# Projecting the context values of the second pair of units one slot earlier, into the other accumulator pool

## The chip, the cores and the metric

The kernel runs on one core of a Trainium2 chip. The time is that of one execution on the device, in microseconds; the time before is the median of three runs. All data are 32-bit floats.

The core has engines that each work through their own queue of instructions in order: TensorE (PE in the profile, with its weight loads under PEld), VectorE (DVE), ScalarE (ACT), GpSimd (POOL), and SyncE (SP), which here only hands out DMA transfers. PE writes its products into banks of accumulator memory (PSUM); a bank can be given to a new product only when DVE or ACT has copied the old one out.

## The reference

One transformer block on `x` of shape (2, 1024, 256) and a context `cond` of shape (2, 154, 192), with 16 heads of 64:

```python
h = _layernorm(x, ln1_g, ln1_b)
x = _attention(h, h, sa_wq, sa_wk, sa_wv, sa_wo, sa_bo) + x
h = _layernorm(x, ln2_g, ln2_b)
x = _attention(h, cond_emb, ca_wq, ca_wk, ca_wv, ca_wo, ca_bo) + x
h = _layernorm(x, ln3_g, ln3_b)
p = h @ ff_w1 + ff_b1
a, gate = (p[..., :D_FF], p[..., D_FF:])
h = a * jax.nn.gelu(gate, approximate=False) @ ff_w2 + ff_b2
return h + x
```

`_attention(xq, xkv, ...)` projects queries from `xq` and keys and values from `xkv`, takes the softmax of the scaled products per head, weighs the values and multiplies by `wo`. The change lies in the second call, context attention: the keys and values come from the 154 rows of the context, and the value projection is `v = cond_emb @ ca_wv`.

## The kernel before, in words

The whole order of work is written out by hand: the instructions go to each engine's queue in the order in which the Python code calls them, and a framework adds the semaphore waits. Three stages follow each other: self attention, context attention (from about 697 us of the span), and the gated feed-forward layer (from about 895 us).

**Units and slots.** A unit is a batch and a pair of heads; there are 16 (`units`, eight per batch). Context attention works on a unit in three slots, since its eight tiles of 128 tokens are taken as 3 + 3 + 2 (`CG`), so there are 48 slots, numbered `c` from 0; `ui, n = divmod(c, 3)` are unit and part. The slots around the change are 5 to 11: slot 5 is the last of unit 1, slots 6, 7 and 8 are unit 2, slots 9, 10 and 11 are unit 3.

**What a slot issues.** `cross_first(c)` puts the scores on PE (L873, tile `sc`) and the row maxima on DVE (L879, `neg`); then what waited in the list `stores` is flushed, that is, copies out of accumulators; then `then()` puts the exponents on ACT (L890, six or four of them, which need the maxima). The call before's `late` puts a reciprocal on DVE (L898, `rden`) and the division on POOL (L901). `cross_drain(c)` transposes the result of slot `c - 2` on DVE (L917). Then comes what is special to the slot. With `n == 0` from unit 3 on, the queries of the next unit are projected (L369, `pq_ca`) and copied out by ACT in the next slot (L384, `q_ca`); in slot 6 two pieces of self attention's output projection stand there instead (L500, `py_sa`, added to `x` by DVE, L507). With `n == 1`, `cross_weigh(c)` weighs the values of the unit two before (L953, `poc`), and DVE copies the sums out (L967, `o_ca`). `cross_regroup` moves the transposed weights to where that product wants them, with eight DMAs on SP (L934).

**Context values.** `context_values(b, pr)` (L820) serves two units at a time, with 256 columns. For the first two pairs it clears a part of the buffer on DVE (L829, `held_v`), multiplies the context by the weights on PE (two matmuls, four passes in the trace, L833, `pv_ca`), and leaves a store that copies the product with two instructions on ACT (L843) and asks for six DMAs (two at L845, which need the copies, and four at L850). The weights (`ca_wv`) are loaded by one DMA on SP (L123). Before, this is called for units 2, 4, 6 and so on in the slot with `n == 1`, ahead of `cross_weigh`.

**Two pools of banks.** `mm_tile` and `sum_tile` each hand out two banks in turn; `ps_s` holds two double banks for scores. `cross_values` (L937) takes the first two quarters of a unit (part 0) in banks of `sum_tile` and the last two (part 1) in banks of `mm_tile`:

```python
po = {a4: (mm_tile if a2 else sum_tile)(f"poc_{ui}_{a4}") for a4 in quarters}
```

So in slot 7 the product `pv_ca` and the two quarters of part 1 all come from `mm_tile`, which has two banks.

Of the kernel before, what the change touches and what calls it, by code (L numbers as in the profile page):

```python
# [18 lines left out]
def tile_transformer_block(ctx: ExitStack, tc: tile.TileContext, a: dict, out: bass.AP):  # L19
# [11 lines left out]
    HP = NPAIR // NQ  # L31
# [38 lines left out]
    def mm_tile(name):  # L70
        return ps_m.tile([P, HB], F32, tag="mm", name=name)
# [54 lines left out]
    def load_slice(name, c0, n, p):  # L126

        own = w[name][:, c0:c0 + n]
        if p != HR:
            return load_rows(wpool, name[3:], f"{name}_{c0}", own, p)  # L130
        tag = "wk" if name == "ca_wq" and c0 // P % 2 else name[3:]
        t = wpool.tile([P, NH, n], F32, tag=tag, name=f"{name}_{c0}")
        for r0 in range(0, P, HR):
            nc.sync.dma_start(out=t[r0:r0 + HR], in_=own.rearrange("(c p) f -> p c f", p=HR))
        return t
# [3 lines left out]
    def load_weights(kind, pr, what):  # L139
        if what != "v":  # L140
            wsl[kind, pr, what] = load_slice(f"{kind}_w{what}", pr * P, P, HR)
        elif pr % 2 == 0:
            wsl[kind, pr, what] = load_slice(
                f"{kind}_w{what}", pr * P, VC, HR if kind == "sa" else CC)
# [446 lines left out]
    def run(piece):  # L591
        done = piece()
        if done is not None:
            (adds if getattr(done, "adds", False) else stores).append(done)
# [6 lines left out]
    def run_work(n, n_side, bank=None, n_sum=0):  # L601

        while n > 0 and work:
            n -= work[0].banks
            run(work.pop(0))
        for _ in range(min(n_side, len(side))):
            needs_bank, needs, fn = side[0]  # L610
            if needs_bank and not bank and n <= 0 or not added.issuperset(needs):
                break
            if needs_bank and not bank:
                n -= 1
            spare["bank"] = bank or mm_tile
            run(fn)
            side.pop(0)
        if not spare["turned"]:
            flush(slow)
        for i in range(min(max(n, 0) + n_sum, len(outs))):  # L620
            spare["out"] = mm_tile if i < n else sum_tile
            run(outs.pop(0))
# [4 lines left out]
    units = [(b, pr) for b in range(B) for pr in range(NPAIR)]  # L627
# [144 lines left out]
    CG = [(t, min(TG, NT - t)) for t in range(0, NT, TG)]  # L772
# [44 lines left out]
                    )  # L817
        return lambda: nc.scalar.copy(ends[:, f:f + n], pe[:, :n])

    def context_values(b, pr):  # L820

        i = (b * NPAIR + pr) // 2
        if i < 2:
            v = vs["own", i] = held_v[:, i].rearrange("p t d -> p (t d)").rearrange(
                "p (n d) -> p n d", d=VC)
            nc.vector.memset(v[:, NM:, :], 0.0)  # L829
        v = vs["ca", b, pr // 2] = vs["own", i % 2]  # L830
        pv = mm_tile(f"pv_ca{b}_{pr}")
        for c in range(2):
            nc.tensor.matmul(  # L833
                pv[:, :VC], lhsT=ctxT[:, c, b * TP:b * TP + P],
                rhs=wsl["ca", pr, "v"][:, c, :], start=(c == 0), stop=(c == 1),
            )
        half, c0 = divmod(pr * P, DA // 2)
        last = (2 * b + half) * KB

        def store():  # L840
            for n in range(NM):
                own = slice(n * QG, (n + 1) * QG)
                nc.scalar.copy(v[own, n, :], pv[own, :VC])  # L843
            later.insert(0, lambda: [
                nc.sync.dma_start(  # L845
                    out=v[(1 - n) * QG:(2 - n) * QG, n, :], in_=v[n * QG:(n + 1) * QG, n, :])
                for n in range(NM)
            ])
            later.insert(1, lambda: [
                nc.sync.dma_start(  # L850
                    out=v[a4 * KB:(a4 + 1) * KB, NM + a4 % 2, :],
                    in_=ends[last:last + KB, c0:c0 + VC])
                for a4 in range(P // KB)
            ])

        return store
# [409 lines left out]
    with tc.manual_schedule():  # L1266
# [59 lines left out]
        for p in range(SA):  # L1326
# [21 lines left out]
            ui, n = divmod(p, 2 * SH)  # L1348
# [6 lines left out]
            if hg == LAG:  # L1355
                f = (ui - NPAIR // 2 - 1) * EC
# [4 lines left out]
                if n == SH + LAG and ui in (0, 1, NU - 1):  # L1361

                    pr = {0: 2, 1: 4, NU - 1: 6}[ui]
# [3 lines left out]
        for c in range(CA):  # L1367
            if c == 1:
                pTc["ring"] = pt_.tile(
                    [P, 2 * NK, QH // 2], F32, tag="pT", name="pT_ca"  # L1370
                ).rearrange("p a b -> p (a b)")[:, :3 * 2 * NB * NT * KB].rearrange(
                    "p (u n j q) -> p u n j q", u=3, n=NB, j=2)
            if c == SH + 1:
                out_pieces("sa", B - 1, NQ - 1, out_order("sa"))
            if c == SH + 1:

                w1, w2, parts = hold_gated()
                add_biases("ca", 0)
                others = later[:] + [lambda: None] * (len(parts) - len(later))
                later[:] = [fn for pair in zip(parts, others) for fn in pair] + others[len(parts):]  # L1380
            ui, n = divmod(c, len(CG))
            nxt = units[ui + 1] if ui + 1 < NU else None
            if n == 0:
                cross_beside(ui)
            elif n == 1 and 1 <= ui < NU - 3:
                load_weights("ca", units[ui + 3][1], "q")
            elif n == 2 and nxt and ui:
                load_weights("ca", nxt[1], "v")
            flush(adds)
            then = cross_first(c)  # L1390
            if c < 2:
                reciprocals(SA - 2 + c)
            flush(stores)
            if c == 1:
                turn_group(SA - 2, 0)
                turn_group(SA - 2, 1)
                scale_rows(SA - 1, 0, 4)
            flush(lates)
            lates.append(then())
            if c == 0:  # L1400
                join(SA - 1)
                turn_group(SA - 3, 1)
            if c == 2:
                turn_group(SA - 1, 0)
                turn_group(SA - 1, 1)
            cross_drain(c)
            if c == 0:
                run(lambda: self_values(2 * NU - 2, 1))
            elif c == 1:
                run(lambda: cross_queries(*units[2]))  # L1410
            elif c == 2:
                run(lambda: cross_queries(*units[3], bank=sum_tile, tag="KT"))
            elif c == 3:
                run(lambda: self_values(2 * NU - 1, 0))
            elif c == 4:
                run(lambda: self_values(2 * NU - 1, 1))
            elif n == 0 and ui:
                if nxt and ui > 2:
                    run(lambda: cross_queries(*nxt))
                else:  # L1420
                    run_work(2, 0)
                run_work(0, 1)
            elif n == 1:

                spare["turned"] = True
                run_work(0, 1, sum_tile if outs else None)
                flush(stores)
                run_work(0, 0, n_sum=1)
                if ui % 2 == 0:
                    run(lambda: context_values(*units[ui]))  # L1430
                run_work(1, 0)
                flush(adds)
                flush(slow)
                flush(stores)
                cross_weigh(c)
            elif n == 2:
                run_work(0, ui != HP, sum_tile if ui == HP + 1 else None)
                if c == SH + 1:
                    run_work(2, 0)
                elif ui == HP:  # L1440
                    wo["ca"] = const.tile([P, NPAIR, D], F32, tag="wo", name="ca_wo")
                    later[1:1] = [lambda i=i: nc.sync.dma_start(
                        out=wo["ca"][:, i, :], in_=w["ca_wo"][i * P:(i + 1) * P, :])
                        for i in range(NPAIR)]
            flush(slow)
            cross_regroup(c)
            for _ in range(min(1 if ui in (HP, HP + 1) else 2, len(later))):
                later.pop(0)()
            if c == CA - 22:
                weighted = [fn for n in range(4) for fn in weight_sums(n)]  # L1450
            if CA - 22 <= c < CA - 10:
                weighted.pop(0)()
            elif c >= CA - 3:
                for n in {CA - 3: (4,), CA - 2: (5, 6), CA - 1: (7,)}[c]:
                    weight_sums(n)[0]()
            if c == CA - 5:
                token_sums(0)
# [7 lines left out]
        for k in range(2 * FU):  # L1465
            c = CA + k
# [17 lines left out]
            while n_left > 0 and sums:  # L1484
                fn, n = sums.pop(0)
# [51 lines left out]
```

## Time and profile before

| | |
|---|---|
| median of 3 runs | 1069.95 us (1069.39 to 1070.63) |
| the profiled execution | 1071.75 us |
| its span (first to last instruction) | 1069.1 us |
| PE busy | 1057.3 us (99%) |
| DVE, ACT, POOL busy | 882.9, 645.3, 774.8 us |
| granted PE clock | 1.0 over the span |

The profile of one execution lists for each engine its instructions in order of time, with the idle time before a group of them and what ended it; the chain of waits follows the work that ended last backwards; and the view of waits adds up who waited for whom. The span leaves out 2.65 us of the profiled execution's own time, and that execution was 1.80 us above the median. Only differences within the span are used below.

### The profile page before, as it was taken

The numbers are of one execution on the slowest core, as the hardware profiler recorded it, in microseconds if no ns is written. First come the engines' busy times: TensorE is split into PE (matmuls) and PEld (weight loads), VectorE is DVE, ScalarE is ACT, GpSimd is POOL, SyncE is SP. The second block draws the span as 40 slices with busy tenths as digits, with TensorE's granted clock in tenths as the row PEclk, the third lists the DMA queues.
The fourth block names the chain that finished last, engine by engine and source line by source line (L and its number), as shares of the span: only waits on it lengthen the run. The fifth ranks groups of instructions, "written<-read, shape, count | busy, mean of one in ns | idle before, by whom it ended". The sixth has DMA issues, their size and how long they took to land.

```text
span 1069.1 us, 48669 instructions
## 1 busy us (share of the span) xinstructions
PE 1057.3 (99%) x20228; PEld 709.8 (66%) x20228; DVE 882.9 (83%) x1321; ACT 645.3 (60%) x2096; POOL 774.8 (72%) x1652
## 2 busy tenths in 40 slices
PE   8999999999999999999999999999999999999998
PEld 6556756655555556657655655576866667788998
DVE  5789999998989989999999899978877887654554
ACT  5766667677666666666777676665666554342221
POOL 2677777778777777777777777676767876499984
PEclk9999999999999999999999999999999999999999
DMA  4132122021021121111102101126776545000000
GB/s 102 38 73 54 29 68 53 25 63 41 22 52 33 34 51 33 40 34 34 45 14 54 44 14 38 33 56 145 173 177 176 123 98 119 11 11 11 21 10 30
DMA packets 86046, 60.95 MB, mean 57 GB/s; under 512 B 32123, under 2 KB 74563, under 8 KB 85827
## 3 DMA queue, kind: packets, MB, share of 16 engines
q1 hardware_dynamic: 84450, 57.07, 22.0%
q8 instruction: 159, 2.61, 1.0%
q10 hardware_dynamic: 1376, 0.79, 0.2%
q14 instruction: 61, 0.49, 0.2%
HBM read 27.91 MB, written 2.10 MB: 28 GB/s over the span
## 4 chain that ended last, share of the span: by engine, by line
PE 92%; DVE 2%; DMA 2%; POOL 2%; SPq 1%; ACT 1%; issue 1%; DVEq 0%; POOLq 0%
PE po L578 20%; PE s L526 20%; PE py_ca L500 5%; PE py_sa L500 5%; PE pk_sa L369 5%; PE pq_sa L369 5%; PE pq_ca L369 5%; PE pv_sa L405 4%; PE poc L953 4%; PE pb L1074 4%; PE pq L1219 4%; PE sc L873 3%; PE pa L1074 2%; PE pc L1074 2%; PE pf L1249 1%; PE ph_ln L286 1%
## 5 line engine op out<-in xcount | busy, mean ns | idle before, releaser
L650 POOL TENSOR_SCALAR p<-p,rd,ee 128x512 f32<-128x512 f32 x512 | 390.4, 768 | 90.4 <-DVE rd L640 89.4
L537 ACT ACTIVATE p<-s,st 128x512 f32<-128x512 f32 x512 | 345.0, 686 | 175.6 <-DVE st L712 172.4
L712 DVE TENSOR_REDUCE st<-s 128x2 f32<-128x1024 f32 x256 | 308.9, 1207 | 59.6 <-issue 20.3
L675 DVE STREAM_TRANSPOSE pT<-p 128x1024 f32<-128x1024 f32 x256 | 302.8, 1220 | 2.1 <-POOL p L650 1.9
L526 PE MATMUL s<-k_sa,q_sa 64*32 64x512 f32 x4096 | 260.3, 591 | 0.8 <-DVE k_sa L390 0.6
L578 PE MATMUL po<-pT,held_v 64*32 64x256 f32 x8192 | 241.9, 376 | 0.4 <-DMA held_v<-held_v 0.4
L578 PEld LDWEIGHTS po<-pT,held_v 64*32 64x32 f32 x8192 | 177.3, 106 | 72.5 <-issue 25.2
L526 PEld LDWEIGHTS s<-k_sa,q_sa 64*32 64x32 f32 x4096 | 90.4, 106 | 91.6 <-issue 48.1
L890 ACT ACTIVATE p<-sc,neg 128x154 f32<-128x154 f32 x256 | 96.1, 404 | 76.1 <-DVE rden L898 73.3
L901 POOL TENSOR_SCALAR p<-p,rden 128x154 f32<-128x154 f32 x256 | 96.8, 399 | 49.2 <-DVE rden L898 49.0
L537 ACT ACTIVATION_READ_ACCUMULATOR p<-s,st 128x1 f32 x512 | 104.1, 203 | 0.0
L555 POOL TENSOR_TENSOR dd<-st 128x8 f32<-128x8 f32 x128 | 25.5, 199 | 71.9 <-DMA st<-st 68.5
L500 PE MATMUL py_ca<-ca_wo,o_ca 128*128 128x256 f32 x256 | 60.2, 383 | 0.0
L369 PE MATMUL pq_ca<-hT_ln,ca_wq 64*64 64x512 f32 (+1 forms) x576 | 59.4, 589 | 0.5 <-DMA ca_wq<-in_L_xattn_ca_wq_dram 0.5
L500 PE MATMUL py_sa<-sa_wo,o_sa 128*128 128x256 f32 x256 | 59.5, 386 | 0.0
L500 PEld LDWEIGHTS py_sa<-sa_wo,o_sa 128*128 128x128 f32 x256 | 47.3, 190 | 18.0 <-issue 5.0
L369 PE MATMUL pk_sa<-hT_ln,sa_wk 64*32 64x512 f32 x960 | 57.6, 590 | 0.4 <-ACT q_sa L384 0.4
L369 PE MATMUL pq_sa<-hT_ln,sa_wq 64*32 64x512 f32 (+1 forms) x976 | 57.7, 586 | 0.0
L879 DVE TENSOR_REDUCE neg<-sc 128x6 f32<-128x924 f32 (+1 forms) x48 | 47.8, 996 | 12.0 <-PE sc L873 11.8
L890 ACT ACTIVATION_READ_ACCUMULATOR p<-sc,neg 128x1 f32 x256 | 56.5, 221 | 0.0
L405 PE MATMUL pv_sa<-sa_wv,hT_ln 64*32 64x256 f32 x1792 | 53.7, 376 | 0.0
L917 DVE STREAM_TRANSPOSE pT_ca<-p 128x480 f32<-128x480 f32 (+1 forms) x96 | 52.9, 587 | 0.8 <-POOL p L901 0.8
(158 smaller groups left out, 1479.0 us busy)
## 6 DMA issues: line engine op xcount, KB each, us to landing
wf<-pT_ca SPq DMA_DIRECT2D x128, 128.0 KB, 2.4
st<-st SPq DMA_DIRECT2D x512, 1.0 KB, 1.8
held_v<-held_v SPq DMA_DIRECT2D x32, 256.0 KB, 4.1
sa_wq<-in_L_xattn_sa_wq_dram SPq DMA_DIRECT2D x32, 128.0 KB, 2.9
sa_wk<-in_L_xattn_sa_wk_dram SPq DMA_DIRECT2D x32, 128.0 KB, 3.2
sa_wv<-in_L_xattn_sa_wv_dram SPq DMA_DIRECT2D x16, 256.0 KB, 4.5
ca_wq<-in_L_xattn_ca_wq_dram SPq DMA_DIRECT2D x32, 128.0 KB, 3.8
wf<-in_L_xattn_ff_w_dram SPq DMA_DIRECT2D x12, 256.0 KB, 3.4
```

The lines of the kernel that those rows point to most:

```text
L369: nc.tensor.matmul(pq[r][f:f + m, at:at + n], lhsT=wt[own, c, f:f + m], rhs=h[own, c, t0:t0 + n], start=(c == 0), stop=(c == NH - 1), tile ...
L405: nc.tensor.matmul(pv[r][f:f + KB, e * VC:(e + 1) * VC], lhsT=h[half, c, t0:t0 + KB], rhs=wt[half, c, :], start=(c == 0), stop=(c == NH - ...
L500: nc.tensor.matmul(py[:, e * D:(e + 1) * D], lhsT=o[:, i, (t + e) * P:(t + e + 1) * P], rhs=wo[kind][:, g * HP + i, :], start=(i == 0), st ...
L526: nc.tensor.matmul(sc[a4 * KB:(a4 + 1) * KB, j, :], lhsT=q[r, c:c + KB], rhs=k[r, h * HB:(h + 1) * HB], start=True, stop=True, tile_positi ...
L537: nc.scalar.activation(pr[:, j, :], sc[:, j, :], AF.Exp, bias=st[:, 0, 0, i, j:j + 1], accum_out=st[:, 0, 1, i, j:j + 1],)
L578: nc.tensor.matmul(po[a2][d:d + KB, :QH // 2], lhsT=v[e][r, t, d:d + KB], rhs=pT[r, d // DH * NK + n, :], start=(t == 0 and e == 0), stop= ...
L650: nc.gpsimd.tensor_scalar(pr[:, j, :], pr[:, j, :], own["rd"][:, c:c + 1], own["ee"][:, 0, c:c + 1], op0=ALU.mult, op1=ALU.mult,)
L675: nc.vector.transpose(halves[h][:, :, c:c + KB], slots[p]["p"][i].rearrange("p j (n k) -> p (j n) k", k=KB))
L712: nc.vector.tensor_reduce(st[:, 0, 0, i, :], sc[i], AX.X, ALU.max, negate=True)
L890: nc.scalar.activation(pr_[:, j, i, :T], sc[:, j, i * T:(i + 1) * T], AF.Exp, bias=neg[:, j, i:i + 1], accum_out=den[:, j, i:i + 1],)
L901: nc.gpsimd.tensor_scalar(pr_[:, j, i, :T], pr_[:, j, i, :T], rden[:, j, i:i + 1], 1.0, op0=ALU.mult, op1=ALU.mult,)
L1074: nc.tensor.matmul(into[:, :BT], lhsT=lhs, rhs=wh[pair][i], start=first, stop=True, skip_group_check=True)
```

## The change

Three edits. `context_values` gets a parameter for the pool its bank comes from. For unit 2 it is called in slot 6 (`n == 0`, `ui == HP`, and `HP` is 2) with `sum_tile`, behind the two pieces of self attention's output projection, and no longer in slot 7; later pairs stay where they are. The weights of that pair are asked for in slot 3 (`c == len(CG)`), and no longer in slot 5.

```diff
-    def context_values(b, pr):
+    def context_values(b, pr, bank=mm_tile):
...
-        pv = mm_tile(f"pv_ca{b}_{pr}")
+        pv = bank(f"pv_ca{b}_{pr}")
...
-            elif n == 2 and nxt and ui:
+            elif n == 2 and nxt and ui > 1:
+                load_weights("ca", nxt[1], "v")
+            if c == len(CG):
                 load_weights("ca", nxt[1], "v")
...
                     run_work(2, 0)
+                if ui == HP:
+                    run(lambda: context_values(*units[ui], bank=sum_tile))
                 run_work(0, 1)
...
-                if ui % 2 == 0:
+                if ui % 2 == 0 and ui > HP:
                     run(lambda: context_values(*units[ui]))
```

In the engines' queues this moves, and changes in number, nothing else: on PE the `pv_ca` matmuls stand ahead of the scores of slot 7 and no longer behind them; on DVE the clearing stands behind the transposes of slot 6 (of scores 4), ahead of two pairs of statistics and two additions to `x`; on ACT the two copies stand ahead of the exponents of slot 7 and no longer behind them; on SP the load of `ca_wv` stands one place earlier, ahead of the two DMAs that load `ca_wq` for unit 4.

## The prediction

> **What bounds the kernel now.** I read the page's busy times and chain first, then the waits of PE, then the chain and the engines' order of time around the slots that the change touches.
>
> ```profile
> span 1069.1 us, 48669 instructions
> PE 1057.3 (99%) x20228; PEld 709.8 (66%) x20228; DVE 882.9 (83%) x1321; ACT 645.3 (60%) x2096; POOL 774.8 (72%) x1652
> PE 92%; DVE 2%; DMA 2%; POOL 2%; SPq 1%; ACT 1%; issue 1%; DVEq 0%; POOLq 0%
> ```
>
> PE is busy 99% of the span and carries 92% of the chain, so a change pays only where PE stands idle, 11.8 us in all. The view of waits, for PE from 690 to 735 us, has one row, and from 735 us to the end two:
>
> ```profile
> PE poc L953 <- ACT held_v L843: 1.4, 1, 1.4
> ...
> PE pb L1074 <- DVE own L1103: 0.7, 1, 0.7
> PE ph_ln L286 <- POOL xn_ln L273: 0.6, 3, 0.2
> ```
>
> The first is the place of the change: in slot 7 PE, weighing the values, waits 1.4 us for ACT's copy of `pv_ca`. The chain there:
>
> ```profile
> 728.43 0.99 PE sc L873 x24
> 729.42 0.02 issue
> 729.45 1.12 DVE neg L879
> 730.57 0.11 DVE rden L898
> 730.67 0.01 issue
> 730.68 2.33 ACT p L890 x12
> 733.01 0.23 ACT held_v L843
> 733.25 0.03 issue
> 733.27 0.38 ACT held_v L843
> ```
>
> The copy is behind the six exponents of slot 7, these behind the maxima, and these behind the scores. PE, which issued `pv_ca` long before, needs its bank for the last quarter of `poc`:
>
> ```profile
> 729.31 1.13 PE L833 MATMUL pv_ca<-ca_wv,ctxT 96*128 96x256 f32 x4
> 730.37 1.09 PE L953 MATMUL poc<-wf,held_v 64*64 64x256 f32 x16
> ...
> 733.69 0.86 PE L953 MATMUL poc<-wf,held_v 64*64 64x256 f32 x10 [1.38 <-ACT held_v L843]
> ```
>
> **A second, hidden gate behind it.** 8 us later weight loads of PE are held up twice, in slot 10, by ACT's copies of the queries, which free the two banks of `mm_tile` for part 1 of the next `poc`:
>
> ```profile
> 741.77 0.19 PEld L953 LDWEIGHTS poc<-wf,held_v 64*64 64x64 f32 x4 [0.21 <-ACT q_ca L384]
> ...
> 742.26 0.41 PEld L953 LDWEIGHTS poc<-wf,held_v 64*64 64x64 f32 x10 [0.29 <-ACT q_ca L384]
> ```
>
> These 0.50 us don't show in the row of PE itself, whose passes overlap. They matter: behind this gate PE's pace is that of ACT's copies, and ACT's that of DVE's maxima. So what the change wins ahead of it counts only as far as DVE wins it too. DVE and ACT in this stretch:
>
> ```profile
> 728.15 1.26 DVE L507 TENSOR_TENSOR x<-py_sa,x 128x512 f32<-128x512 f32 x2
> 729.45 1.12 DVE L879 TENSOR_REDUCE neg<-sc 128x6 f32<-128x924 f32 x1
> 731.50 0.48 DVE L829 MEMSET held_v<- 128x512 f32 x1
> 731.91 0.37 DVE L242 BATCH_NORM_STATS2 st_ln<-x 128x6 f32<-128x256 f32 x1
> ...
> 734.88 0.80 DVE L967 COPY o_ca<-poc 128x256 f32<-128x256 f32 x2 [1.22 <-PE poc L953]
> 735.77 0.80 DVE L879 TENSOR_REDUCE neg<-sc 128x4 f32<-128x616 f32 x1
> ...
> 737.71 1.08 DVE L879 TENSOR_REDUCE neg<-sc 128x6 f32<-128x924 f32 x1
> ...
> 730.68 0.39 ACT L890 ACTIVATE p<-sc,neg 128x154 f32<-128x154 f32 x1 [2.27 <-DVE rden L898]
> ...
> 741.10 1.11 ACT L384 ACTIVATE q_ca<-pq_ca 128x512 f32<-128x512 f32 x2
> ```
>
> From 734.88 on DVE has no idle time until slot 10 is through; its place there decides when the copies at 741.10 come.
>
> **The change part by part.**
>
> *The product moves ahead of the scores of slot 7.* Nothing is added on PE: the same four passes. But the scores, and DVE's maxima behind them, come later by what `pv_ca` takes. In the next pair of units it stands between two pieces of an output projection, as it will here:
>
> ```profile
> 752.24 1.03 PE L833 MATMUL pv_ca<-ca_wv,ctxT 96*128 96x256 f32 x4
> 753.11 1.89 PE L500 MATMUL py_ca<-ca_wo,o_ca 128*128 128x256 f32 x8
> ```
>
> 753.11 less 752.24 is 0.87 us. The maxima start at 729.45 + 0.87 = 730.32. In its old place it held PE 730.37 - 729.31 = 1.06 us.
>
> *The copy moves ahead of the exponents of slot 7.* `pv_ca` ends near 729.3, and ACT stands idle for 2.27 us up to 730.68; the copies (0.76 us) lie in that gap, end near 730.1, and cost nothing. Without that cover they would delay the exponents by 0.76. The exponents themselves start 0.87 later.
>
> *The bank.* `pv_ca` takes one bank of `sum_tile`, and the second quarter of part 0 takes it over, about 0.2 us after part 0 starts at 730.3; the copy is then out. Part 1 finds both banks of `mm_tile` emptied by the additions to `x`, which DVE ends near 729.8. So the 1.38 us are gone and `poc` runs its 48 passes through, until about 733.05 at the 2.75 us that they take undisturbed later:
>
> ```profile
> 780.70 2.75 PE poc L953 x48
> ```
>
> What is late next: scores 9 need the double bank of scores 7, so the exponents of slot 7, which end at 730.32 + 1.23 + 2.33 = 733.88, while PE is through with scores 8 at about 733.6: a new wait of 0.3 us.
>
> *The clearing* moves from 731.50 to about 727.1 on DVE. There it pushes the statistics and the two additions (728.15) by 0.41, to an end at 729.8, which is still ahead of the maxima at 730.32: nothing. In its old place it gives back 0.41 (731.50 to 731.91).
>
> *Sum at the gate.* DVE goes from the maxima of slot 7 to those of slot 8 in 735.77 - 729.45 = 6.32 us; without the clearing (0.41) and without the wait for the late quarter (1.22) in 4.69. They start at 730.32 + 4.69 = 735.01, that is 0.76 earlier. The maxima of slot 9 (737.71), the exponents of slot 9 and ACT's copies at 741.10 follow without a gap of more than 0.6 us in front of them and come 0.76 earlier. PE can't run away from DVE before that: `pq_ca` needs the banks that DVE's copies of `poc` leave, at 734.88 + 0.80 now and 0.76 earlier then. So PE waits at the gate for its 0.50 of now or somewhat longer, and leaves it 0.76 earlier. After it the view shows only the two short waits quoted at first, on engines that follow PE themselves, so I let the 0.76 reach the end.
>
> *SP and POOL.* The order of the DMAs, the time to landing of `ca_wv` and of the regrouping (part 6 of the page), and POOL's division for slot 6:
>
> ```profile
> 706.62 1.37 SPq L134 DMA_DIRECT2D ca_wq<-in_L_xattn_ca_wq_dram  x2
> 708.03 0.60 SPq L123 DMA_DIRECT2D ca_wv<-in_L_xattn_ca_wv_dram  x1
> 719.63 5.64 SPq L934 DMA_DIRECT2D wf<-pT_ca  x8
> ...
> 733.27 1.16 SPq L845 DMA_DIRECT2D held_v<-held_v  x2
> 734.53 5.31 SPq L934 DMA_DIRECT2D wf<-pT_ca  x8
> ...
> DMA to landing us min/median/max: 4.2/4.2/4.2
> ...
> wf<-pT_ca SPq DMA_DIRECT2D x128, 128.0 KB, 2.4
> ...
> 730.76 2.27 POOL L901 TENSOR_SCALAR p<-p,rden 128x154 f32<-128x154 f32 x6 [3.02 <-DVE rden L898]
> ```
>
> `ca_wv` issues near 706.6 and lands at 711, some 17 us before it is used at 728.4; `ca_wq` comes 0.6 later, for a use in slot 9. SP then idles till 719.63: both are free. The two transfers at L845 wait for the copy and go out near 730.2; the eight behind them then wait for the transposes of slot 7, some 732.4, not 734.53. They issue in 5.31 and land 2.4 later, at 740.1; part 1 at the gate wants them at 741. Without the earlier copy they would land at 742.2 as now, and take the gate over. POOL issues no DMA and keeps its order; its division for slot 6 comes 0.87 later, to an end at 733.9, and DVE's transposes need it only behind the maxima of slot 8, at 735.8.
>
> The bounds of what no row shows, the gain that survives the gate: above, 1.38 + 0.50 + 0.19 (1.06 - 0.87) = 2.07; below, nothing, if DVE loses what it wins. I take 0.76, from DVE's own rows. Against the profiled execution (1071.75, span 1069.1) that makes 1070.99 and 1068.34; against the median of the runs, 1.80 below that execution, 1069.95 - 0.76 = **1069.2 us**.
>
> **The rivals.**
>
> *All of the stall stays won* (PE alone sets the pace): 1.38, plus 0.19 for the cheaper place of `pv_ca`, give 1069.95 - 1.57 = 1068.4; with the gate's 0.50 too, 1067.9. For it: PE's 99%. Against it: the two waits for `q_ca`. The Trainium skill, page "TensorEngine Tiling (Array Packing)", section "Key Properties", says that changing the tiling mode drains TensorE; the new order has two changes of tile shape fewer (64\*64, 96\*128, 64\*64 was the old one). By that rule the 0.19 is real and belongs to this rival; the trace's 1.06 against 0.87 agrees.
>
> *DVE gives it all back*: the chain of 4.69 us meets a new wait of 0.76 (for POOL's division, say, or because the additions slip behind 730.3): 1069.95. Against it: both have 0.5 us to spare or more.
>
> *Slower: the copy frees the bank late.* If ACT copied only after the exponents of slot 7, PE would now stand in the second quarter, not in the fourth. The exponents would end at 733.9, the copy at 734.65, and the 44 passes left (2.5 us) at 737.2, against 735.1 now: 2.1 slower, 1072.05. It decides from a copy that ends after 732.6. Against it: the copy precedes the exponents in ACT's queue, and `pv_ca` has its weights early.
>
> *No effect* since `pv_ca` isn't where the time goes is excluded by the row of 1.38 us.
>
> **How the numbers follow.** My forecast 0.55, all of the stall 0.22, nothing left 0.11, the late copy 0.07, something unseen 0.05. The forecast's own range is 0.4 to 1.2 us of gain, 1068.75 to 1069.55. The range given takes in the upper end of the first rival, 1067.9, and the second with the spread of the three runs (1070.63): 1070.7. It leaves out the late copy and the unseen. About 0.2%, 2.1 us, is what a measurement of this kernel can tell from no change. Faster by more needs the whole of the bound of 2.07 and a little: 0.11, half of the first rival's chance. Slower by more: the late copy and part of the unseen, 0.09. Within: 0.80.
>
> **What would show it.** Right: no idle PE ahead of `poc` in slot 7; `held_v` copied on ACT before the exponents of slot 7, inside its gap; maxima of slot 7 about 0.87 later than now and those of slot 8 about 0.76 earlier, both counted from the end of `py_sa`; a short wait of scores 9 for ACT; weight loads of `poc` in slot 10 still waiting for `q_ca`, by 0.5 to 0.9 us. Wrong: those loads not waiting (then the first rival), DVE idle between the maxima of slots 7 and 8, or a wait of `poc` for `held_v` in part 0. A shift that arises outside slots 6 to 10 would make all of this reasoning irrelevant to the result.

## The result and the profile after

The changed kernel takes 1068.05 us (median of 22 runs, 1066.69 to 1069.11) against 1069.83 us of the kernel before beside it (22 runs): a ratio of 0.9985, with a 95% interval of 0.9979 to 0.9991, so 1.0 to 2.3 us less. The forecast was 0.76 us less, 1069.2 us.

The profiled execution after has a span of 1065.1 us, 4.0 us under that before. That difference must not be read as the gain. Cut at two places of PE's order of time, at the first scores of slot 6 and at the first product of the next pair of units (slot 13), it falls apart:

| stretch (us) | before | after | less |
|---|---|---|---|
| start to scores of slot 6 | 723.77 | 720.93 | 2.84 |
| scores of slot 6 to product of slot 13 (called L below) | 28.47 | 27.26 | 1.21 |
| product of slot 13 to the end | 316.86 | 316.91 | -0.05 |

The first stretch has the same code in both but for the place of one load, which is tested below, and in the eight other profiles of this study it lies between 720.22 and 723.55 us, whatever the kernel: the 2.84 us can't be put down to the change. L and the last stretch repeat within a few hundredths (below). So the trace gives 1.21 us, inside the interval of the times.

The waits of PE from 690 to 735 us, after:

```profile
PE sc L873 <- ACT p L890: 0.5, 1, 0.5
```

The 1.4 us for `held_v` are gone; 0.5 us of another wait have come. PE's order of time around the change, after:

```profile
720.93 1.02 PE L873 MATMUL sc<-kT,q_ca 64*64 64x154 f32 x24
721.88 3.72 PE L500 MATMUL py_sa<-sa_wo,o_sa 128*128 128x256 f32 x16
725.43 1.03 PE L833 MATMUL pv_ca<-ca_wv,ctxT 96*128 96x256 f32 x4
726.39 1.02 PE L873 MATMUL sc<-kT,q_ca 64*64 64x154 f32 x24
727.23 1.16 PE L953 MATMUL poc<-wf,held_v 64*64 64x256 f32 x16
...
731.10 1.02 PE L873 MATMUL sc<-kT,q_ca 64*64 64x154 f32 x24 [0.46 <-ACT p L890]
...
748.19 1.03 PE L833 MATMUL pv_ca<-ca_wv,ctxT 96*128 96x256 f32 x4
```

No `poc` waits in slot 7; scores 9 (731.10) wait 0.46 us, for the exponents of slot 7. DVE, ACT and the weight loads of PE in the same stretch, after:

```profile
727.48 1.12 DVE L879 TENSOR_REDUCE neg<-sc 128x6 f32<-128x924 f32 x1 [0.38 <-PE sc L873]
728.51 0.18 DVE L898 RECIPROCAL rden<-den 128x6 f32<-128x6 f32 x1
728.61 0.86 DVE L917 STREAM_TRANSPOSE pT_ca<-p 128x320 f32<-128x320 f32 x2
729.40 0.38 DVE L242 BATCH_NORM_STATS2 st_ln<-x 128x6 f32<-128x256 f32 x1
...
730.44 1.39 DVE L967 COPY o_ca<-poc 128x256 f32<-128x256 f32 x4
731.74 0.79 DVE L879 TENSOR_REDUCE neg<-sc 128x4 f32<-128x616 f32 x1
...
726.50 0.76 ACT L843 COPY held_v<-pv_ca 64x256 f32<-64x256 f32 x2 [0.91 <-PE pv_ca L833]
728.71 0.39 ACT L890 ACTIVATE p<-sc,neg 128x154 f32<-128x154 f32 x1 [1.45 <-DVE rden L898]
...
737.07 1.11 ACT L384 ACTIVATE q_ca<-pq_ca 128x512 f32<-128x512 f32 x2
...
737.74 0.20 PEld L953 LDWEIGHTS poc<-wf,held_v 64*64 64x64 f32 x4 [0.56 <-ACT q_ca L384]
738.22 0.41 PEld L953 LDWEIGHTS poc<-wf,held_v 64*64 64x64 f32 x10 [0.29 <-ACT q_ca L384]
```

DVE has no idle time between the maxima of slots 7 and 8, ACT's copy lies in a gap, and in slot 10 the weight loads wait for ACT's query copies by 0.85 us instead of 0.50.

### The profile page after: what moved, and what is told of

The parts are those of the page before. It is cut to its first block, busy times and chain, and to the rows that moved or that the text cites. A ratio compares the mean times of both kernels' runs of the same rounds, so it can differ in the third digit from the quotient of the medians.

```text
span 1065.1 us, 48669 instructions
## 1 busy us (share of the span) xinstructions
PE 1055.6 (99%) x20228; PEld 707.7 (66%) x20228; DVE 882.5 (83%) x1321; ACT 647.3 (61%) x2096; POOL 778.4 (73%) x1652
## 4 chain that ended last, share of the span: by engine, by line
PE 90%; DVE 3%; POOL 2%; DMA 2%; SPq 1%; issue 1%; ACT 1%; DVEq 0%; POOLq 0%; ACTq 0%
PE po L578 19%; PE s L526 19%; PE py_ca L500 5%; PE py_sa L500 5%; PE pk_sa L369 5%; PE pq_sa L369 5%; PE pq_ca L369 4%; PE pv_sa L405 4%; PE poc L953 4%; PE pb L1074 4%; PE pq L1219 4%; PE sc L873 3%; PE pa L1074 2%; PE pc L1074 2%; PE pf L1249 1%; PE ph_ln L286 1%
## 5 line engine op out<-in xcount | busy, mean ns | idle before, releaser
L526 PE MATMUL s<-k_sa,q_sa 64*32 64x512 f32 x4096 | 255.8, 591 | 0.8 <-DVE k_sa L390 0.6
L578 PE MATMUL po<-pT,held_v 64*32 64x256 f32 x8192 | 238.9, 376 | 0.0
L526 PEld LDWEIGHTS s<-k_sa,q_sa 64*32 64x32 f32 x4096 | 87.4, 106 | 93.1 <-issue 46.8
L500 PEld LDWEIGHTS py_ca<-ca_wo,o_ca 128*128 128x128 f32 x256 | 47.4, 190 | 8.2 <-issue 1.9
```

Of the source, the lines that this page charges most:

```text
L500: nc.tensor.matmul(py[:, e * D:(e + 1) * D], lhsT=o[:, i, (t + e) * P:(t + e + 1) * P], rhs=wo[kind][:, g * HP + i, :], start=(i == 0), st ...
L526: nc.tensor.matmul(sc[a4 * KB:(a4 + 1) * KB, j, :], lhsT=q[r, c:c + KB], rhs=k[r, h * HB:(h + 1) * HB], start=True, stop=True, tile_positi ...
L578: nc.tensor.matmul(po[a2][d:d + KB, :QH // 2], lhsT=v[e][r, t, d:d + KB], rhs=pT[r, d // DH * NK + n, :], start=(t == 0 and e == 0), stop= ...
```

## The experiments

Theory A is the prediction's: the stall for the bank is what was won, and what of it lasts is set by DVE's way to slot 9 and ACT's query copies behind it. The two measures are L and, counted from the first scores of slot 6, the start of the maxima of slot 8.

| kernel | L | maxima of slot 8 | scores of slot 6 at | slot 13 to end | time against before, same chip (95%) |
|---|---|---|---|---|---|
| before | 28.47 | 12.00 | 723.77 | 316.86 | |
| before, again | 28.49 | 12.02 | 721.95 | 316.86 | |
| changed | 27.26 | 10.81 | 720.93 | 316.91 | 0.9985 (0.9979 to 0.9991) |
| changed, again | 27.24 | 10.81 | 723.55 | 316.91 | 0.9987 (0.9978 to 0.9996) |
| only the load earlier | 28.48 | 12.01 | 721.99 | 316.93 | one run |
| without the earlier load | 27.26 | 10.82 | 720.22 | 317.02 | one run |
| only the other pool | 31.43 | 14.99 | 720.84 | 316.93 | 1.0027 (1.0017 to 1.0037) |
| only the earlier slot | 28.49 | 12.03 | 721.29 | 316.92 | 0.9999 (0.9990 to 1.0008) |
| changed, clearing twice | 27.77 | 11.34 | 722.82 | 316.91 | 0.9999 (0.9990 to 1.0008) |
| changed, copies shared | 26.58 | 10.15 | 720.75 | 316.97 | 0.9982 (0.9973 to 0.9991) |

### The load of the weights

Only the earlier request, the rest as before:

```diff
-            elif n == 2 and nxt and ui:
+            elif n == 2 and nxt and ui > 1:
+                load_weights("ca", nxt[1], "v")
+            if c == len(CG):
                 load_weights("ca", nxt[1], "v")
```

> Of the change only the earlier request for the weights is kept; the product stays in slot 7 with a bank of mm_tile. Measure L for all runs: from the first scores of slot 6 to the first product of the next pair of units (slot 13) on PE; it is 28.47 us in the kernel before and 27.26 in the changed one. Theory A (the stall for the bank is what was won, cut short by DVE's order of work up to slot 10): the weights were never late, so L stays 28.4 to 28.5 and the 1.38 us of idle PE in slot 7 stay. Rival B (the moved transfers are part of the gain): L falls by 0.2 us or more.

L is 28.48 us and the stall has its 1.38 us:

```profile
731.92 0.86 PE L953 MATMUL poc<-wf,held_v 64*64 64x256 f32 x10 [1.38 <-ACT held_v L843]
```

And the change without that edit:

```diff
-            elif n == 2 and nxt and ui > 1:
-                load_weights("ca", nxt[1], "v")
-            if c == len(CG):
+            elif n == 2 and nxt and ui:
                 load_weights("ca", nxt[1], "v")
```

> The change without the earlier request: product in slot 6, bank of sum_tile, weights asked for in slot 5 as before. Theory A: SP runs far ahead and issues the load near 708 us, it lands 15 us before its use; L is that of the changed kernel, 27.2 to 27.3 us. Rival B: PE waits for ca_wv in slot 6 and L is above 27.5 us.

L is 27.26 us. SP's order of time there:

```profile
703.26 1.38 SPq L134 DMA_DIRECT2D ca_wq<-in_L_xattn_ca_wq_dram  x2
704.68 0.60 SPq L123 DMA_DIRECT2D ca_wv<-in_L_xattn_ca_wv_dram  x1
```

Though asked for two slots later in the code, the load leaves SP at 704.68, since SP has nothing to wait for by then; PE uses it 20 us later. The edit is worth nothing either way; rival B falls.

### The pool without the slot

The product stays in slot 7, with a bank of `sum_tile`, and the earlier load:

```diff
-                if ui % 2 == 0:
-                    run(lambda: context_values(*units[ui]))
+                if ui % 2 == 0:
+                    run(lambda: context_values(*units[ui], bank=sum_tile if ui == HP else mm_tile))
```

> The product stays in slot 7 behind its scores, but takes its bank from sum_tile. Theory A: the copy still comes behind the exponents of slot 7, and now the second quarter of the weighing waits for it, not the fourth: PE idles about 3.0 us and not 1.38; L rises to 29.4 to 29.9 us, the whole run by about 1.1 us. Rival C (the bank's pool is what won, not the place): L is near 27.3 us.

The direction is as expected, and the pool alone is not what wins; but L rose by 2.96 us, more than twice what I expected. The stall has the expected kind, with 2.67 us (about 3.0 expected):

```profile
727.45 0.65 PE L953 MATMUL poc<-wf,held_v 64*64 64x256 f32 x4
730.77 0.87 PE L953 MATMUL poc<-wf,held_v 64*64 64x256 f32 x10 [2.67 <-ACT held_v L843]
```

PE resumes 9.93 us after the scores of slot 6, and 9.92 in the kernel before; with 44 and not 20 passes left, 24 x 0.057 = 1.4 us are accounted for. The rest is in the stages of this run (columns: the stretch, its length, busy time of PE, PEld, DVE, ACT and POOL with their instructions, granted PE clock (1.00 is its full rate), DMA share, GB/s):

```profile
728.00:730.00 2.00, 0.09 (x2) 0.00 (x0) 1.87 (x7) 2.00 (x13) 2.00 (x6) 1.00 0.00 0
730.00:731.00 1.00, 0.23 (x4) 0.21 (x8) 0.10 (x1) 0.69 (x3) 0.85 (x4) 1.00 0.00 0
731.00:732.00 1.00, 1.00 (x24) 0.70 (x20) 0.05 (x1) 0.00 (x0) 0.23 (x1) 0.94 0.26 66
732.00:733.00 1.00, 1.00 (x16) 0.67 (x12) 0.79 (x2) 0.00 (x0) 0.00 (x0) 0.50 0.41 94
733.00:734.00 1.00, 1.00 (x12) 0.55 (x10) 0.01 (x1) 0.00 (x0) 0.00 (x0) 0.50 0.55 111
734.00:735.00 1.00, 1.00 (x18) 0.86 (x14) 0.42 (x1) 0.00 (x0) 0.00 (x0) 0.50 0.39 84
735.00:736.00 1.00, 1.00 (x33) 1.00 (x28) 0.60 (x2) 0.00 (x0) 0.00 (x0) 0.85 0.88 182
736.00:737.00 1.00, 1.00 (x23) 0.82 (x19) 1.00 (x3) 0.25 (x1) 0.17 (x1) 1.00 0.93 205
```

Behind the wait the granted clock is one half for some 3.4 us, which costs at most half of that, 1.7 us; the 2.96 us less the 1.4 of the passes leave 1.6. The last section returns to this.

### The slot without the pool

The product moves to slot 6, with a bank of `mm_tile`:

```diff
-                    run(lambda: context_values(*units[ui], bank=sum_tile))
+                    run(lambda: context_values(*units[ui]))
```

> The product moves to slot 6, but takes a bank of mm_tile. Theory A: that bank holds the output projection's third piece, which DVE adds to x only behind the statistics of slot 6; PE waits for it at pv_ca by 0.8 to 1.0 us, the maxima of slot 7 come later by as much, and L is 28.0 to 28.4 us, so most of the gain is gone. Rival D (the place alone is what wins, the pool is of no account): no wait at pv_ca, L 27.2 to 27.4 us.

```profile
726.91 1.13 PE L833 MATMUL pv_ca<-ca_wv,ctxT 96*128 96x256 f32 x4 [0.95 <-DVE x L507]
...
732.68 1.02 PE L873 MATMUL sc<-kT,q_ca 64*64 64x154 f32 x24 [0.57 <-ACT p L890]
```

The wait is 0.95 us, scores 9 wait another 0.57, and L is 28.49, slightly above the 28.0 to 28.4 expected: nothing of the gain is left. The times agree (0.9999). So slot and pool win only together, and rival D falls too.

### Work on DVE behind the maxima of slot 7

In the changed kernel, the clearing is done a second time in its old place:

```diff
                 run_work(0, 0, n_sum=1)
...
+                if ui == HP:
+                    nc.vector.memset(vs["own", 1][:, NM:, :], 0.0)
                 run_work(1, 0)
```

> The changed kernel, with the clearing on DVE done a second time in its old place, behind the transposes of slot 7 (half a microsecond of DVE work that nothing needs). Theory A (behind slot 7 PE follows ACT's query copies, which follow DVE): the maxima of slots 8 and 9 come 0.5 us later, the weight loads in slot 10 wait 0.5 us longer, L rises from 27.26 to 27.7 or 27.8 us. Rival E (PE alone sets the pace, and the whole stall of 1.38 us less 0.17 elsewhere is what was won): L stays at 27.2 to 27.3 us.

```profile
730.50 0.86 DVE L917 STREAM_TRANSPOSE pT_ca<-p 128x320 f32<-128x320 f32 x2
731.42 0.48 DVE L1436 MEMSET held_v<- 128x512 f32 x1
731.83 0.37 DVE L242 BATCH_NORM_STATS2 st_ln<-x 128x6 f32<-128x256 f32 x1
```

L rises to 27.77 us, by 0.51: half a microsecond of work on DVE whose result nobody needs costs PE half a microsecond. From the start of the transposes to the statistics DVE now takes 1.33 us, and 0.79 without the clearing: it costs 0.54. ACT's query copies come at 16.66 us after the scores of slot 6 and not 16.14, 0.52 later. One part of the expectation was wrong: the weight loads in slot 10 wait 0.58 and 0.29, hardly longer than in the changed kernel (0.56 and 0.29).

```profile
733.96 0.62 PEld L369 LDWEIGHTS pq_ca<-hT_ln,ca_wq 64*64 64x64 f32 x9 [0.24 <-DVE o_ca L967]
...
740.15 0.19 PEld L953 LDWEIGHTS poc<-wf,held_v 64*64 64x64 f32 x4 [0.58 <-ACT q_ca L384]
...
740.64 0.41 PEld L953 LDWEIGHTS poc<-wf,held_v 64*64 64x64 f32 x10 [0.29 <-ACT q_ca L384]
```

PE is held ahead of them already: at `pq_ca` the weight loads wait 0.24 us for DVE's copies of `poc`, and PE ends part 0 of the weighing in slot 10 at 17.21 us after the scores of slot 6, against 16.70 in the changed kernel. What holds it for the rest of these 0.51 us, the rows don't show. The times of this kernel (0.9999 of the kernel before, 0.9990 to 1.0008) don't resolve it: the 0.70 us by which its L is below that of the kernel before lie within that interval.

The opposite, as work taken off DVE: two of its four copies of the first weighed unit go to ACT.

```diff
-                copy = nc.scalar.copy if pools and a4 // 2 else nc.vector.tensor_copy
+                copy = nc.scalar.copy if (pools or ui == 0) and a4 // 2 else nc.vector.tensor_copy
```

> The changed kernel, with two of DVE's four copies of the first weighed unit (slot 7) given to ACT, which idles 1.60 us there. Theory A: DVE is through 0.65 us earlier, the maxima of slot 8 come at 10.2 us after the first scores of slot 6 and not 10.81, the waits of the weight loads in slot 10 shrink from 0.85 to about 0.2 us, and L falls to 26.6 or 26.8 us; the run gains another 0.5 to 0.65 us. Rival E: L stays at 27.2 to 27.3 us.

```profile
730.26 0.72 DVE L967 COPY o_ca<-poc 128x256 f32<-128x256 f32 x2
730.90 0.79 DVE L879 TENSOR_REDUCE neg<-sc 128x4 f32<-128x616 f32 x1
...
730.74 0.67 ACT L967 COPY o_ca<-poc 128x256 f32<-128x256 f32 x2
731.81 0.39 ACT L890 ACTIVATE p<-sc,neg 128x154 f32<-128x154 f32 x1 [0.40 <-DVE rden L898]
...
736.23 1.11 ACT L384 ACTIVATE q_ca<-pq_ca 128x512 f32<-128x512 f32 x2
```

The maxima of slot 8 come at 10.15 and not 10.81 us after the scores of slot 6, the query copies at 15.48 and not 16.14, the waits of the weight loads in slot 10 are gone from the view, and L falls to 26.58, by 0.68. PE's own rows list no idle time in slot 10 of the changed kernel, and yet there was this much to win: "a change pays only where PE stands idle" doesn't hold there. The median is 1067.58 us against 1069.62 before and 1068.58 of the changed kernel on the same chip. In the trace it beats both; in the times its interval (0.9973 to 0.9991) is clear of the kernel before and overlaps that of the changed one.

With both signs, rival E falls: on this stretch PE doesn't set the pace alone. The path can be followed through all ten profiles: from ACT's first query copy of slot 10 to the first product of slot 13 it is 11.10 to 11.14 us in every one, while L goes from 26.58 to 31.43.

### Both kernels again

The same code as the changed kernel, and as the kernel before:

> The changed kernel once more, beside the one before on the same chip. Theory A: L is 27.26 us and the time from slot 13 to the end 316.9 us again, so that the local gain of 1.21 us is all there is: 1.2 us less in the time, within the spread of what lies before slot 6. Rival F (the change also gains outside slots 6 to 13): the time differs by 1.6 us or more again.

> The kernel before once more. Theory A: L is 28.47 us again, with 1.38 us of idle PE in slot 7, and the granted clock stays at 1.00 behind that wait; the start of slot 6 lies anywhere from 720 to 724 us, as in runs of the other kernels. Rival F: the start of slot 6 is above 723 us again, as in the first profile of this kernel and in no profile of another.

L is 27.24 and 28.49, the last stretch 316.91 and 316.86. The time differs by 1.0 us in the medians (1068.58 and 1069.62; ratio 0.9987, 0.9978 to 0.9996), which holds 1.21. And the changed kernel's start of slot 6 at 723.55, that of the kernel before at 721.95, have the reverse order of the first two profiles: that stretch shows no gain that follows the change. The spans of all executions can be used too: on this chip they have a mean of 1067.70 us before (27 of them) and 1066.46 after (11), a difference of 1.24 us, and the times have means that differ by 1.19. Nothing speaks for rival F, but the interval still holds its 1.6 us: it is not excluded.

## Why the prediction was right, and what was off

- *The stall of 1.38 us goes, since the copy falls into ACT's gap.* Right: the copy takes 0.76 us with 1.45 us of idle time left behind it, and both halves of the move are needed.
- *The scores and maxima of slot 7 come 0.87 later.* Measured from the scores of slot 6, the maxima start at 5.68 before and 6.55 after, 0.87 later. That the figure is met to the hundredth is luck: it was taken from a row in which `pv_ca` stands between two pieces of an output projection, and here the scores come behind it. It takes 726.39 - 725.43 = 0.96, and the projection ahead of it 0.09 to 0.10 less than before. The new wait of scores 9 is 0.46 us (expected 0.3). PE's rows of the kernel before:

```profile
723.77 1.02 PE L873 MATMUL sc<-kT,q_ca 64*64 64x154 f32 x24
724.71 3.72 PE L500 MATMUL py_sa<-sa_wo,o_sa 128*128 128x256 f32 x16
728.36 1.02 PE L873 MATMUL sc<-kT,q_ca 64*64 64x154 f32 x24
```

- *DVE's stretch from the maxima of slot 7 to those of slot 8 in 4.69 us* is the term that was mis-sized: it takes 731.74 - 727.48 = 4.26. The sum therefore gave 0.76 where the trace shows 1.21. Two parts of it, in these rows of the kernel before:

```profile
730.58 0.86 DVE L917 STREAM_TRANSPOSE pT_ca<-p 128x320 f32<-128x320 f32 x2
...
732.94 0.72 DVE L967 COPY o_ca<-poc 128x256 f32<-128x256 f32 x2
```

  The clearing cost 0.54 there (730.58 to 731.91, against 0.79 us for the same stretch after), and not the 0.41 I took from its own start to its successor's; the second clearing confirmed 0.54. And DVE's four copies took 735.77 - 732.94 = 2.83 with an idle time of 1.22 between the pairs, so 1.61 without it, but take 1.30 when they run without a break (730.44 to 731.74). Here the recorded idle time is less than what the interruption costs. 0.13 + 0.31 = 0.44, and 0.76 + 0.44 = 1.20: the maxima of slot 8 come 1.19 earlier and L is shorter by 1.21.
- *The gate in slot 10 decides what lasts.* That DVE's work decides it is shown by the two experiments on it, in both directions. That it does so by the weight loads of this gate is shown by the shared copies alone, where their waits go and L falls by 0.68; with the second clearing PE was late ahead of the gate. The wait of 0.85 us is in the range expected.
- *All of the stall stays won* gave 1068.4, nearer to the measured median than my 1069.2, yet as a mechanism it is refuted by the two experiments on DVE's work; and in the changed kernel PE waits at scores 9 (0.46 us), and its weight loads wait longer at the gate (by 0.35). The cheaper place of `pv_ca` that this rival drew on is there: from scores 7 and product to `poc` PE took 730.37 - 728.36 = 2.01 and takes 727.23 - 725.43 = 1.80; from the scores of slot 6 to `poc` it took 6.60 and takes 6.30. The sizes alone can't tell the two accounts apart: 0.30, and 1.38 less the new 0.46, make 1.22 as well. Only the experiments on DVE's work do. The count of "two changes of tile shape fewer" doesn't fit the shapes as the rows print them: 128\*128, 64\*64, 96\*128, 64\*64 has three changes and 128\*128, 96\*128, 64\*64 has two. It fits if 96\*128 and 128\*128 count as one, and the rows are in favour of that: the four passes of `pv_ca` take 0.87 us between products of 128\*128, 0.96 ahead of 64\*64 and 1.06 between 64\*64.
- *SP's moves are free.* Right, shown for the load. The eight transfers of the regrouping went out 2.15 us earlier than before (2.13 expected):

```profile
726.89 1.16 SPq L845 DMA_DIRECT2D held_v<-held_v  x2
729.54 5.30 SPq L934 DMA_DIRECT2D wf<-pT_ca  x8
```

- *The late copy* as the slower rival did not occur, but the pool tried alone shows its kind. I reckoned 2.1 us for PE standing in the second quarter, with the scores 0.87 later; in the kernel with the pool alone they are not later, and what is left of that sum is 2.1 - 0.87 = 1.2 us, or 1.4 by the count of passes above. L rose by 2.96 us and the medians by 2.83: the sum left out the half clock behind such a wait.
- What stays open: the medians differ by 1.78 and by 1.04 us, and the 1.21 us of the trace lie in both intervals; a gain or loss elsewhere of a few tenths can't be excluded by the times, though no stretch of the traces shows one that goes with the change.

## What to carry to other kernels

Don't let a bank be taken by a product whose copy stands behind other work on the copying engine: look for a slot where the copy falls into a gap, and for a pool whose bank is free there; here either half alone won nothing or lost. When a wait goes, look for the next place where the winner waits for the same engines, and add up their work from there: half a microsecond more or less on an engine that is "not the bottleneck" moved the end of this stretch by just that. And where profiles of two runs differ in stretches with the same code, compare the stretch that the change touches, not the spans.

## What the runs showed of the hardware

A wait of PE of 2.67 us (3.13 us between weight loads) was followed, from 1.1 us after its end on, by a granted clock of 0.50 for some 3.4 us. In the kernel with the pool alone, eight of ten executions had a mean clock under 1.00, with spans of 1068.3 to 1071.8 us; the two at 1.00 had 1067.7 and 1068.7. A wait of 1.38 us did this at most rarely: one of 46 executions of the kernel before, in the two later comparisons, showed 0.999, and none of 33 of the changed kernel. The Trainium skill, page "TensorE: Matmul & The Clock Gate", section "What's actually happening", gives two states, half and full rate, and an idle window of about 3.4 us that runs freely of the kernel; the half rate and the chance from run to run agree, but here a gap shorter than that window was enough.

PE doesn't take its passes strictly in the order of its queue. At the end of slot 10 of the changed kernel four passes of the next scores start at 739.15, ahead of two of `poc` at 739.36 that stand before them in the code:

```profile
739.15 0.43 PE L873 MATMUL sc<-kT,q_ca 64*64 64x154 f32 x4
739.36 0.38 PE L953 MATMUL poc<-pT_ca,held_v 64*64 64x256 f32 x2
```
